# A state-space block with adaptive norms: the input of later halves loaded with channels on partitions and normed in place, the gates' rows moved to other engines, and the output weight's load issued earlier

## The chip, the cores and the metric

The kernel runs on one core of one Trainium2 chip. The metric is device time in microseconds of one execution, all loads and stores included. Three runs of the kernel before the change took 735.45, 736.16 and 738.33 us, so the median is 736.16 us. The profile comes from one more execution on the chip; the predicted time is that of the changed kernel on the same inputs.

## The reference

The input `x` is 4 batches of 512 tokens with 512 channels, all in float32. A conditioning row per batch gives six vectors, and the block adds two branches to `x`, an SSD (Mamba2) mixer and a layer with binarised weights:

```python
mod = (silu(c) @ wmod).reshape(4, 6, 1, -1)
sa, ca, ga, sb, cb, gb = (mod[:, i] for i in range(6))
ga = (2 * (ga >= 0) - 1) * maximum(abs(ga), 0.25)      # gb likewise
h = layernorm(x) * (1 + ca) + sa
x = x + ga * attn(h)
h = layernorm(x) * (1 + cb) + sb
x = x + gb * (h @ (sign(weight) * mean(abs(weight), axis=1, keepdims=True)).T + bias)
```

`attn` projects `h` to 3136 columns: 2048 for x, B and C, 1024 for z, 64 for dt. The 2048 go through a causal convolution of four taps and a silu. Then a scan over chunks of 128 tokens runs for 64 heads of 16 channels and 8 groups with a state of 64: within a chunk `Y_diag = C B^T * exp(segsum(-dt)) * X`, across chunks the carried states times their decays. `D * x / dt` is added, the result is multiplied by `silu(z + z_bias)`, and a projection takes 1024 channels back to 512. All inputs reach the kernel as float32 arrays that the host may lay out anew (transposed, split over partitions), without arithmetic.

## The kernel before

**Tiles.** The 2048 tokens are worked off in eight halves `h` of T = 256 tokens, two to a batch. A half has two chunks of 128 tokens, and each chunk has four pairs of head groups, which makes eight units (h, chunk, pair) in a half. One step of the outer loop (lines 844–863) finishes one unit and begins the one two steps on.

**Stages of a half.** `load_x` (75) brings two tiles of 128 tokens x 512 channels. `f_norm` (307) calls `layer_norm` (289): VectorE takes the statistics (295, 296) and adds the epsilon (297), GpSimd raises to the power −1/2 (298), VectorE normalises in place (300). `f_hT` (335) turns the normed tiles on TensorE (`turned_x`, eight transposes of 128x128, line 330, into two PSUM tiles `phT`), and ScalarE scales and shifts four blocks of 128x256 out of PSUM into `hT` (347). GpSimd fills the three columns ahead of `hT` that the convolution needs. `f_dt` (353) projects the 64 dt columns (`pa`, 368), works out dt and its running sums on VectorE and ScalarE, and writes the sums, their exponentials and the reciprocals to DRAM (`sums_d`, `e_d`, `r_d`). They come back by loads that lay one head's row over all 128 partitions.

`conv_pair` (434–459) projects two blocks of channels (`pp_x`, `pp_B`, `pp_C`, line 434: four matmuls of 128x128 by 259 columns each), takes the last tap on ScalarE (450), the other three on VectorE (454), a tanh on ScalarE (458) and the silu's product on VectorE (459). `f_z` (516–522) does the same for z without a convolution. `f_xt` and `f_Bt` turn x and B to tokens on partitions.

**Units.** Stage 0 loads the sums of one pair of groups into one of four buffers `decay0`–`decay3` (lines 541 and 542, a load of 256 KB and one of 128 KB for each buffer, SP's queue). ScalarE takes exponentials (549), TensorE works out C B^T (`gy`), VectorE masks it (`gm`, 621) and multiplies decay by it (625), and TensorE multiplies the product by x (`py`, 212 and 215, two halves of 16 matmuls each). `pst` is the product for the carried states.

**Tail of a chunk.** `tail1` (739–747) projects back to 512 channels (`po`, 16 matmuls by 512 columns), multiplies by the first gate, adds the input (loaded once more as `xr`) and norms; `tail2` turns and scales; `tail3` (775–779) multiplies by the binarised weight `bwT` (`pf`), by the second gate, adds and stores.

**Once, during the first two halves.** `late_mods` (233) makes the four remaining rows of the modulation in PSUM tile `pg`, copies them to SBUF (243), turns two of them (247, 248) and then computes the gates: five VectorE operations (256–260), the last with the FFN's bias `brow` (loaded on SP, 255), and three writes to `gate_d` in DRAM (262, SP's queue). `load_gates` reads them back over all partitions per batch into `gates`, a tile for which `room` was used before. `load_wout` (264) loads the output weight, 2 MB, after `pg`'s matmuls have read the data whose place it takes. `signs(o)` (269) loads a block of 128 rows of the FFN weight (`fw`, 256 KB), reduces its absolute values to `alpha` (274) and takes signs; `turned_signs(o)` (281) transposes it into `bwT`.

**What sets the order.** The lists FRONT, FIRST and SECOND (787–810) name the step at which each of these functions is called: for halves 2 to 7 the load of x at step 1, the norm at 2, `hT` and dt at 3, B and C from 4, x from 5, z from 8, counted in the units of the half before. `behind` pins a function behind the latest projection of its half on TensorE. Lines 822–829 place `late_mods` at step 1, `load_wout` at 2, `signs(o)` at `o // 2 + 2` and `turned_signs(o)` at `o // 2 + 5`. A scheduler then orders the instructions of each engine from the program's order, priorities and buffers: PSUM tiles come from five "mm" buffers and two others, SBUF tiles from pools (x and xr share three, `hT` has two, `rr` two). Each engine, SP and GpSimd as issuers of DMAs too, works its own list in order and stands where the next instruction isn't ready. All loads named here are issued by SP; the writes of the halves after the first by GpSimd.

Of the kernel before, what the change touches and what calls it, by code (L numbers as in the profile page):

```python
# [11 lines left out]
F32 = mybir.dt.float32  # L12
# [4 lines left out]
P = 128  # L17
# [23 lines left out]
def adaln_mamba_block(  # L41
    ctx: ExitStack,
    tc: tile.TileContext,
    x: bass.AP,
    w_inT: bass.AP,
# [27 lines left out]
    xs_of = {}  # L73

    def load_x(h, queue=nc.sync):
# [5 lines left out]
        xs_of[h] = tiles  # L81

# [37 lines left out]
    sums_d = dram.tile([NHALF, 2, NH, CH], F32, name="sums_d")  # L120
    e_d = dram.tile([NHALF, 2, NH, CH], F32, name="e_d")
# [111 lines left out]
    def late_mods(h):  # L233
# [26 lines left out]
        nc.vector.tensor_mul(ab[second, :], sg[second, :], brow[second, :])  # L260
        for i, v in enumerate((sg[0:B, :], sg[second, :], ab[second, :])):
            nc.sync.dma_start(gate_d[:, i, :], v)
# [26 lines left out]
    def layer_norm(tiles, name, into=None):  # L289
# [3 lines left out]
        rs = wk.tile([P, n], F32, tag=f"rs{n}", name=f"rs_{name}")  # L293
# [4 lines left out]
        nc.gpsimd.tensor_tensor(rs, rs, mhalf[:, :n], ALU.pow)  # L298
        for j, t in enumerate(tiles):
# [5 lines left out]
    H = [dict(B={}, C={}, xt={}, xs={}, bt={}, z={}) for _ in range(NHALF)]  # L305
# [29 lines left out]
    def f_hT(h, turned=None):  # L335
        b = h // HPB

        hT = wk.tile([P, NK, KS - 1 + T], F32, tag="hT", name=f"hT_{h}")
# [4 lines left out]
        for d2 in range(NK // 2):  # L343
# [562 lines left out]
```

## Time and profile before

| what | value |
|---|---|
| median of three runs | 736.16 us |
| profiled execution | 737.38 us, of which 735.7 us are the span of the profile |
| mean granted clock of TensorE | 0.993 |
| instructions | 15007 |
| bytes moved by DMA | 99.24 MB, 135 GB/s in the mean |
| one later half | 86.0 or 87.3 us, in turns |
| ScalarE's decay exponentials (549) | 960 of 395 ns, 293.9 us |
| VectorE's decay products (625) | 120 of 1341 ns, 160.8 us |
| transposes of x on TensorE (330) | 64 of 273 ns |
| normalisations of x (300) | 16, median 546 ns |
| scaling into `hT` (347) | 32, median 564 ns |

The span is the time from the first to the last profiled instruction; 1.7 us of the execution lie outside it. A line of a timeline gives start and duration in microseconds, engine and line of the code, operation, output from inputs, partitions and elements, and how many instructions are put together (xN); in brackets stands the idle time of that engine just before and what ended it. A line of the windows gives the stretch, its length, each engine's busy time and number of instructions, TensorE's granted clock (1.00 is full speed), the mean busy share of the DMA engines and the rate. In the chain of waits each line is a start, a duration and the work that everything after it waited for. PEld is TensorE's weight load, which overlaps its matmuls; SPq is SP's own queue of DMA issues. A line of DMA issues gives the number, the size of each, and the median time from issue to landing.

### The profile page before, as it was taken

What the parts mean: (1) busy time and instruction counts of PE and PEld (TensorE: products, weight loads), DVE (VectorE), ACT (ScalarE), POOL (GpSimd) and SP (SyncE); (2) the same over time, 40 slices, a digit from 0 to 9 for tenths busy, and PEclk for the clock granted to TensorE, in tenths of its full rate; (3) what the DMA queues carried; (4) which work ended last, traced back from release to release, by engine and by line L of the source; (5) the groups of instructions that cost most, each with busy time, mean ns of one, the idle gap of its engine ahead of it and who ended that gap; (6) DMA issues with size and microseconds to landing.
All of it is one profiled execution on the core that took longest, in us unless ns stands there. A gap on an engine that the chain in (4) does not pass through costs nothing.

```text
span 735.7 us, 15007 instructions
## 1 busy us (share of the span) xinstructions
PE 700.4 (95%) x5196; PEld 500.8 (68%) x5196; DVE 599.5 (81%) x1170; ACT 522.0 (71%) x1507; POOL 254.8 (35%) x297
## 2 busy tenths in 40 slices
PE   6999979899999999999999999999999999999997
PEld 3786746666677666677677666776667866677754
DVE  3869888876998678986899768996799867996995
ACT  2467658748696697785976787865968768788941
POOL 4021323444243332343223342433414332333652
PEclk9999989999999999999999999999999999999999
DMA  8991693535555256444644256552564537457720
GB/s 279 328 291 41 204 208 85 135 98 142 127 132 144 63 155 137 102 115 102 159 116 130 53 116 168 142 137 53 140 132 114 130 86 176 116 150 151 142 69 29
DMA packets 119067, 99.24 MB, mean 135 GB/s; under 512 B 73984, under 2 KB 97152, under 8 KB 118992
## 3 DMA queue, kind: packets, MB, share of 16 engines
q1 hardware_dynamic: 117808, 96.39, 52.3%
q0 software_dynamic: 896, 1.38, 0.7%
q8 instruction: 41, 0.67, 0.4%
q10 hardware_dynamic: 288, 0.52, 0.2%
q14 instruction: 34, 0.28, 0.1%
HBM read 92.47 MB, written 5.79 MB: 134 GB/s over the span
## 4 chain that ended last, share of the span: by engine, by line
PE 65%; ACT 16%; DVE 9%; DMA 4%; issue 4%; POOL 1%; SPq 1%; ACTq 0%; DVEq 0%; POOLq 0%
PE po L739 14%; PE pp_x L434 11%; PE pp_z L434 10%; ACT decay L549 9%; PE pp_C L434 7%; PE pp_B L434 5%; PE pf L775 3%; PE py L212 2%; PE py L215 2%; DVE decay L625 2%; ACT h L759 2%; DVE u_x L454 2%; DMA fw<-in_ffn_w 2%; ACT win L549 2%; PE gy L215 2%
## 5 line engine op out<-in xcount | busy, mean ns | idle before, releaser
L549 ACT ACTIVATE decay<-decay,st 128x128 f32<-128x128 f32 x960 | 293.9, 395 | 4.2 <-DMA decay<-sums_d 3.7
L625 DVE SCALAR_TENSOR_TENSOR decay<-decay,gm 128x1024 f32<-128x1024 f32 x120 | 160.8, 1341 | 50.3 <-ACT decay L549 47.2
L434 PE MATMUL pp_x<-hT,win 128*128 128x259 f32 x512 | 120.7, 390 | 7.3 <-DVE u_C L454 7.3
L434 PE MATMUL pp_z<-hT,win 128*128 128x256 f32 x512 | 118.1, 383 | 0.0
L434 PEld LDWEIGHTS pp_x<-hT,win 128*128 128x128 f32 x512 | 96.9, 193 | 25.2 <-ACT decay L549 7.7
L739 PE MATMUL po<-wout,z 128*128 128x512 f32 x256 | 113.8, 595 | 0.0
L434 PEld LDWEIGHTS pp_z<-hT,win 128*128 128x128 f32 x512 | 94.3, 189 | 16.3 <-issue 3.5
L675 POOL TENSOR_TENSOR z<-yt,z 128x256 f32<-128x256 f32 x62 | 62.9, 1015 | 76.1 <-DVE yt L674 57.8
L454 DVE SCALAR_TENSOR_TENSOR u_x<-pp_x,cw,u_x 128x256 f32<-128x256 f32 x192 | 83.6, 474 | 1.3 <-ACT u_x L450 0.7
L739 PEld LDWEIGHTS po<-wout,z 128*128 128x128 f32 x256 | 47.5, 190 | 53.1 <-issue 52.4
L672 POOL TENSOR_TENSOR yt<-yt,xs 128x256 f32<-128x256 f32 x46 | 41.4, 899 | 106.3 <-DVE yt L671 78.6
L507 POOL TENSOR_TENSOR xs<-u_x,rr 128x512 f32<-128x512 f32 x32 | 42.7, 1334 | 79.2 <-DVE u_x L459 61.3
L516 ACT ACTIVATE uz<-pp_z,zb 128x256 f32<-128x256 f32 x64 | 27.5, 470 | 59.0 <-PE pp_z L434 59.0
L215 PE MATMUL py<-decay,xpad 128*32 128x128 f32 x1680 | 66.3, 276 | 0.0
L434 PE MATMUL pp_B<-hT,win 128*128 128x259 f32 x256 | 63.5, 396 | 2.7 <-ACT decay L549 1.9
L434 PE MATMUL pp_C<-hT,win 128*128 128x259 f32 x256 | 59.6, 384 | 1.1 <-DVE u_x L454 1.1
L775 PE MATMUL pf<-bwT,h 128*128 128x512 f32 (+1 forms) x136 | 59.0, 578 | 1.4 <-ACT h L759 1.3
L434 PEld LDWEIGHTS pp_B<-hT,win 128*128 128x128 f32 x256 | 47.4, 193 | 14.5 <-ACT decay L549 3.1
L450 ACT ACTIVATE u_x<-pp_x,cb,cw 128x256 f32<-128x256 f32 x64 | 35.3, 560 | 30.5 <-PE pp_x L434 30.4
L434 PEld LDWEIGHTS pp_C<-hT,win 128*128 128x128 f32 x256 | 47.8, 189 | 9.4 <-PE pn L424 1.4
L679 POOL TENSOR_TENSOR xd<-xpad,st 128x256 f32<-128x256 f32 x48 | 34.1, 727 | 55.8 <-PE pst L215 28.3
L212 PE MATMUL py<-decay,xpad 128*32 128x128 f32 x240 | 47.4, 279 | 3.2 <-issue 2.2
(157 smaller groups left out, 1080.9 us busy)
## 6 DMA issues: line engine op xcount, KB each, us to landing
decay<-sums_d SPq DMA_DIRECT2D x120, 256.0 KB
decay<-sums_d SPq DMA_DIRECT2D x120, 128.0 KB
rr<-r_d SPq DMA_DIRECT2D x64, 128.0 KB
e<-e_d SPq DMA_DIRECT2D x96, 64.0 KB
win<-in_w_inT SPq DMA_DIRECT2D x4, 1024.0 KB
xr<-in_x SPq DMA_DIRECT2D x16, 256.0 KB
res<-o SPq DMA_DIRECT2D x15, 256.0 KB
x<-in_x SPq DMA_DIRECT2D x14, 256.0 KB
```

What stands on the lines that cost most here:

```text
L212: first = products[0]()
L215: product()
L434: last = mm(pm, win[:, k, col : col + P], H[h]["hT"][:, k, lo:], start=(k == 0), stop=(k == NK - 1))
L450: nc.scalar.activation(u[:, j, :], pm[:, KS - 1 :], AF.Identity, bias=cb[:, t : t + 1], scale=cw[:, t, KS - 1 : KS])
L454: nc.vector.scalar_tensor_tensor(u[:, j, :], pm[:, k : k + T], cw[:, t, k : k + 1], u[:, j, :], ALU.mult, ALU.add)
L507: nc.gpsimd.tensor_tensor(xs, xc, rr, ALU.mult)
L549: nc.scalar.activation(ets[r][:, i, :], ets[r][:, i, :], AF.Exp, bias=H[h]["st"][:, hd : hd + 1], scale=-1.0)
L625: nc.vector.scalar_tensor_tensor(ets[r], ets[r], 1.0, bc_mid(gm[:, r, :], HPG), ALU.min, ALU.mult)
L672: ew.tensor_add(t, t, xs)
L675: ew.tensor_mul(zg, t, zg)
L739: last_po = mm(po, H[h]["z"][g // 2][:, g % 2, c * CH : (c + 1) * CH], wout[:, g, :], start=(g == 0), stop=(g == NKI - 1))
L775: mm(pf, h2[:, k, :], bwT[:, k, cols], start=(k == 0), stop=(k == NK - 1))
```

## The change

**The load and the norm.** The host hands over a second copy of the input, `xT`, with channels on partitions. For halves 1 to 7, `load_x` also loads the half's block of it straight into the tile `hT`. `f_norm` then only takes the statistics from the token-major tiles and writes means and factors to a new DRAM array `stat_d`, from GpSimd's queue. `f_hT` reads them back over all partitions (`mr`, 256 KB, SP's queue), subtracts and multiplies in place on VectorE over all four blocks, and ScalarE scales and shifts each block in place. The eight transposes of these halves and their PSUM tiles go. Half 0 keeps its path.

**The gates.** The five VectorE operations become one on VectorE, one on ScalarE and three on GpSimd, called at step 2 as `late_gates`, behind `load_wout` in the program. The three writes to `gate_d` go to GpSimd's queue. `brow` is loaded early with the other late loads, and the tiles lie in `room`.

**The order.** With the gates' writes off SP and `load_wout` ahead of them, the output weight's load is behind `pg`'s matmuls only. `signs` moves from step `o // 2 + 2` to `o // 2 + 4`, `turned_signs` from `o // 2 + 5` to `o // 2 + 6`.

```diff
     def load_x(h, queue=nc.sync):
...
         xs_of[h] = tiles
+        if h > 0:
+            hT = wk.tile([P, NK, KS - 1 + T], F32, tag="hT", name=f"hT_{h}")
+            queue.dma_start(hT[:, :, KS - 1 :], xT[:, :, h * T : (h + 1) * T])
+            H[h]["hT"] = hT
...
+    stat_d = dram.tile([NHALF, 2, T], F32, name="stat_d")
...
+        nc.sync.dma_start(brow[second, :], ffn_b.partition_broadcast(B))
...
-        g = row[0:64, :]
-        sg = wk.tile([64, DM], F32, tag="h2", name="sg")
-        ab = wk.tile([64, DM], F32, tag="h2", name="ab")
-        brow = wk.tile([64, DM], F32, tag="th", name="brow")
-        second = slice(32, 32 + B)
-        nc.sync.dma_start(brow[second, :], ffn_b.partition_broadcast(B))
-        nc.vector.tensor_scalar(sg, g, 0.0, 2.0, ALU.is_ge, ALU.mult)
-        nc.vector.scalar_tensor_tensor(ab, g, -1.0, g, ALU.mult, ALU.max)
-        nc.vector.tensor_scalar(ab, ab, 0.25, None, ALU.max)
-        nc.vector.scalar_tensor_tensor(sg, sg, -1.0, ab, ALU.add, ALU.mult)
-        nc.vector.tensor_mul(ab[second, :], sg[second, :], brow[second, :])
+        late_row.append(row)
+
+    late_row = []
+    second = slice(32, 32 + B)
+    brow = room[0:64, 2, :]
+
+    def late_gates(h):
+        g = late_row.pop()[0:64, :]
+        sg, ab = room[0:64, 0, :], room[0:64, 1, :]
+        nc.vector.tensor_scalar(sg, g, 0.0, 0.5, ALU.is_ge, ALU.subtract)
+        nc.scalar.activation(ab, g, AF.Abs)
+        nc.gpsimd.tensor_scalar(ab, ab, 0.25, 2.0, ALU.max, ALU.mult)
+        nc.gpsimd.tensor_tensor(sg, sg, ab, ALU.mult)
+        nc.gpsimd.tensor_tensor(ab[second, :], sg[second, :], brow[second, :], ALU.mult)
         for i, v in enumerate((sg[0:B, :], sg[second, :], ab[second, :])):
-            nc.sync.dma_start(gate_d[:, i, :], v)
+            nc.gpsimd.dma_start(gate_d[:, i, :], v)
...
     def f_norm(h):
+        ms = wk.tile([P, 2, 2], F32, tag="ms", name=f"ms_{h}")
+        mv = statistics(xs_of.pop(h), f"a{h}", ms[:, 1, :])
+        nc.gpsimd.tensor_copy(ms[:, 0, :], mv[:, :, 0])
+        with nc.allow_non_contiguous_dma(reason="a token's value is on its partition"):
+            nc.gpsimd.dma_start(stat_d[h].rearrange("q (j p) -> p q j", p=P), ms)
+
+    def f_first(h):
         H[h]["xn"] = xs_of.pop(h)
         layer_norm(H[h]["xn"], f"a{h}", H[h]["xn"])
-
-    def f_first(h):
-
-        f_norm(h)
...
     def f_hT(h, turned=None):
...
-        for d2 in range(NK // 2):
-            pt = turned[d2] if turned else turned_x(h, d2)
-            for q in range(2):
-                dt = 2 * d2 + q
-                nc.scalar.activation(
-                    hT[:, dt, KS - 1 :], pt[:, q, :], AF.Identity,
-                    bias=modT[:, 0, dt, b : b + 1], scale=modT[:, 1, dt, b : b + 1],
-                )
-        H[h]["hT"] = hT
+        now = hT[:, :, KS - 1 :]
+        if not turned:
+            mr = wk.tile([P, 2, T], F32, tag="rr", name=f"mr_{h}")
+            nc.sync.dma_start(mr, stat_d[h].partition_broadcast(P))
+            nc.vector.tensor_sub(now, now, bc_mid(mr[:, 0, :], NK))
+            nc.vector.tensor_mul(now, now, bc_mid(mr[:, 1, :], NK))
+        for dt in range(NK):
+            nc.scalar.activation(
+                now[:, dt, :], turned[dt // 2][:, dt % 2, :] if turned else now[:, dt, :], AF.Identity,
+                bias=modT[:, 0, dt, b : b + 1], scale=modT[:, 1, dt, b : b + 1],
+            )
...
             at(2, load_wout)
+            at(2, late_gates, h)
             for o in range(NK):
-                at(o // 2 + 2, signs, o)
+                at(o // 2 + 4, signs, o)
     for o in range(NK):
-        at(o // 2 + 5, behind, 1, turned_signs, o)
+        at(o // 2 + 6, behind, 1, turned_signs, o)
...
         "x": np.ascontiguousarray(np.asarray(L0_attn_input_).reshape(B * L, DM)),
+        "xT": cols(np.asarray(L0_attn_input_).reshape(B * L, DM).T),
```

`statistics` is the first part of the old `layer_norm` (295–298) as a function of its own, which writes the factors into a tile given to it and returns means and variances; `layer_norm` now calls it.

More of the change, by code (lines that the diff above doesn't have):

```diff
@@ L44, in adaln_mamba_block @@
     x: bass.AP,
+    xT: bass.AP,
     w_inT: bass.AP,
@@ L73, in adaln_mamba_block @@
     xs_of = {}
+    H = [dict(B={}, C={}, xt={}, xs={}, bt={}, z={}) for _ in range(NHALF)]
     def load_x(h, queue=nc.sync):
@@ L286, in turned_signs, with statistics @@
         nc.scalar.activation(bwT[:, :, o * P : (o + 1) * P], pt, AF.Copy, scale=2.0 / DM)
-    def layer_norm(tiles, name, into=None):
+    def statistics(tiles, name, rs):
         n = len(tiles)
@@ L298, in layer_norm @@
         nc.gpsimd.tensor_tensor(rs, rs, mhalf[:, :n], ALU.pow)
+        return mv
+    def layer_norm(tiles, name, into=None):
+        n = len(tiles)
+        rs = wk.tile([P, n], F32, tag=f"rs{n}", name=f"rs_{name}")
+        mv = statistics(tiles, name, rs)
         for j, t in enumerate(tiles):
@@ L302, in layer_norm @@
             )
-    H = [dict(B={}, C={}, xt={}, xs={}, bt={}, z={}) for _ in range(NHALF)]
     def f_norm(h):
+        ms = wk.tile([P, 2, 2], F32, tag="ms", name=f"ms_{h}")
[4 more added lines that the diff above has]
+    def f_first(h):
         H[h]["xn"] = xs_of.pop(h)
         layer_norm(H[h]["xn"], f"a{h}", H[h]["xn"])
-    def f_first(h):
-        f_norm(h)
         for xp in xpads:
@@ L336, in f_hT @@
         b = h // HPB
-        hT = wk.tile([P, NK, KS - 1 + T], F32, tag="hT", name=f"hT_{h}")
+        if turned:
+            hT = H[h]["hT"] = wk.tile([P, NK, KS - 1 + T], F32, tag="hT", name=f"hT_{h}")
+        hT = H[h]["hT"]
         if h % HPB == 0:
```

1 line of the change is left out of this document (removed).

## The prediction

> **What bounds the kernel now.** I read the page's busy shares and its chain of waits first:
>
> ```profile
> PE 700.4 (95%) x5196; PEld 500.8 (68%) x5196; DVE 599.5 (81%) x1170; ACT 522.0 (71%) x1507; POOL 254.8 (35%) x297
> ...
> PE 65%; ACT 16%; DVE 9%; DMA 4%; issue 4%; POOL 1%; SPq 1%; ACTq 0%; DVEq 0%; POOLq 0%
> ```
>
> TensorE is the bound: 700.4 of 735.7 us. The change can win the 35 us in which it idles and the time of instructions that go, no more. Then the windows, by stage: the second half's start, and one whole later half (184.2 to 270.2), with the columns PE, PEld, DVE, ACT, POOL, granted clock, DMA share, GB/s.
>
> ```profile
> 84.00:98.00 14.00, 9.93 (x105) 7.99 (x104) 12.16 (x29) 7.54 (x19) 5.82 (x8) 0.99 1.04 279
> 98.00:110.00 12.00, 10.60 (x46) 7.20 (x47) 10.30 (x23) 7.28 (x22) 1.34 (x2) 0.73 0.92 210
> 184.20:249.40 65.20, 64.59 (x432) 46.84 (x430) 59.07 (x122) 47.59 (x137) 20.47 (x23) 1.00 0.47 113
> 249.40:270.20 20.80, 19.93 (x199) 14.04 (x195) 13.39 (x22) 16.96 (x52) 9.52 (x13) 1.00 0.49 124
> ```
>
> In the long projection stretch PE idles 0.61 us of 65.2 and VectorE is busy 59.07 (91%), so VectorE has 6.1 us to spare there. Only the second half's start loses much. The windows of 2 us and the chain say by what:
>
> ```profile
> 96.00:98.00 2.00, 0.00 (x0) 0.00 (x0) 1.68 (x5) 1.20 (x2) 0.00 (x0) 0.91 1.10 281
> 98.00:100.00 2.00, 0.59 (x2) 0.53 (x3) 2.00 (x7) 2.00 (x8) 0.00 (x0) 0.50 1.02 294
> ```
> ```profile
> 83.06 13.38 DMA fw<-in_ffn_w
> ...
> 106.70 7.08 PE po L739 x16
> ```
> ```profile
> 72.66 0.60 SPq L262 DMA_DIRECT2D gate_d<-sg  x2
> ...
> 81.79 0.41 SPq L265 DMA_DIRECT2D wout<-in_w_outT  x1
> ```
>
> The first FFN weight block, issued behind the 2 MB output weight, lands 13.4 us later. VectorE's in-order queue waits on it, and PE stands from 94.05 to 99.41, then runs at a granted clock of 0.50 until about 105. On SP the output weight stood behind the gates' writes, the last at 77.66.
>
> Last, PE's timeline where one half passes into the next:
>
> ```profile
> 179.06 1.09 PE L330 MATMUL phT<-ident,x 128*128 128x128 f32 x8
> 180.99 0.27 PE L212 MATMUL py<-decay,xpad 128*32 128x128 f32 x1 [0.84 <-issue]
> ...
> 181.97 0.44 PE L368 MATMUL pa<-hT,win 128*64 128x128 f32 x4 [0.34 <-ACT hT L347]
> ...
> 184.19 2.02 PE L434 MATMUL pp_B<-hT,win 128*128 128x259 f32 x8
> ```
> ```profile
> 181.50 1.65 DVE L625 SCALAR_TENSOR_TENSOR decay<-decay,gm 128x1024 f32<-128x1024 f32 x1
> ```
>
> The eight transposes and the two gaps after them are 1.09 + 0.84 + 0.34 = 2.27 us. But a py half at 183.25 waits for the decay product that VectorE ends at 183.15, so not all of this is the transposes' own.
>
> **The change part by part.** *Transposes off PE (halves 2 to 7, six passages).* At most 2.27 us each. The last decay exp on ScalarE ends at 181.4, the product at 183.15, both untouched, so the second py half stays near 183.25. Ahead of it two of the eight pp_B matmuls can now run, and pa without its wait; the remaining pp_B ends near 186.5 instead of 187.8. I take −1.3 each: −7.8. Bounds: 0 (the four hT activations, 1.91 us, and the decay exps keep ScalarE's order as the limit) and −2.27.
>
> *VectorE's share.* Per half two 128x512 normalisations go (0.546 each, −1.09); a subtract and a multiply over 128x1024 come. No row has that form; an undelayed 128x1024 product takes 1.22 (L625), a mean one 1.34, two 128x512 sums 1.36. At 1.22 that is 2.44 − 1.09 = +1.35 a half. It falls into the 91% stretch, whose first quarter has VectorE busy 96% (15.57 of 16.20 us from 184.2). PE waits for VectorE there only through the conv, with five PSUM buffers between; I take a third, +0.4, times six: +2.4. Bounds 0 (slack of 6.1 us covers it) and 1.35 (2.2 with both operations at the 1.65 seen above).
>
> *The second half's start.* Before, x was normalised at 75–76.6, transposed, and pa ran at 77.87. Now the order of instructions puts one long chain there: bn_aggr 69.7; GpSimd raises to −1/2 (2.55 us here before, 71.79 to 74.34, 0.71 elsewhere); the new copy (0.19, by the 191 ns of the copy in L342) and ScalarE's Abs with GpSimd's clamp (about 0.7) lie beside it; then the write of means and factors to DRAM, 512 pieces of 4 bytes; then mr's load from SP; subtract, multiply, hT's first activation, pa. The output weight's load is let go at about 69 instead of 81.8, so this write meets it. The same kind of write under that load before:
>
> ```profile
> e_d<-es POOLq DMA_DIRECT2D x1, 64.0 KB, 8.4
> ```
>
> Elsewhere it lands in 1.9 (median of seven). I take 8.4: issue 73.5, landed 82. Bounds 1.8 and 8.5; no row has 4-byte pieces. Then mr, 256 KB, 3.9 to 5.0 by the decay loads in the chain (bounds 1.9 and 8.5, as for the write): 86. Two VectorE passes 2.4, an activation 0.56: pa at about 89. PE's order has nothing to put ahead of it: pt_xt ends at 75.1, so PE idles 13.9 us where it idled 2.8 with its transposes, then runs some 3.3 us more than its time at half clock. Against that, the weight blocks are no longer behind the output weight when asked for: the 5.36 us stop and the 3 us lost at half clock go. Together 11.1 + 3.3 − 8.4 = +6.0; one py half stands behind the output projection now (−0.6): the projection starts at 112.1 instead of 106.7, +5.4. Half of it I expect back, because all four decay exps lie ahead of the gap and VectorE has little queued, so the conv chain enters the next stretch with everything prepared: about +2.5. Bounds −1 (the write at 1.9: 5.4 − 6.5) and +9 (the load at 8, nothing caught up).
>
> Here a row and a rule meet. The row: GpSimd's power took 2.55 us against 0.71 while VectorE ran its gate product and a decay product beside it,
>
> ```profile
> 71.79 2.55 POOL L298 TENSOR_TENSOR rs_a<-rs_a,mhalf 128x2 f32<-128x2 f32 x1
> ```
>
> but DMAs from GpSimd's queue land in 1.9 with VectorE 81% busy. The Trainium skill, "SBUF — State Buffer", section "SBUF: two separate sides", speaks against the new write's queue: descriptors of a GpSimd-issued DMA are written by GpSimd's cores, and VectorE operations that hold the shared port keep them out, 620 ns becoming about 3100. By the page alone the write would come 2.5 us later and the total be 2.5 us higher. I go by the row.
>
> *At no cost.* Gates: VectorE loses 0.68 + 0.41 + 0.67 + 0.99 (L257–L260) and keeps one of 0.42; GpSimd gets about 1.3 + 1.3 + 1.0, ScalarE one Abs; GpSimd is 35% busy and the gates are first read at the output projection (113.8). Should gate_d be late, up to 1 us there. The three gate writes leave SP for GpSimd's queue at 0.5 to 0.8 each. SP: fourteen issues more of 0.4 to 0.6 us, in an engine that mostly waits; mr's wait on SP holds the e and gates loads behind it, used microseconds later, and in halves 2 on the statistics are written long ahead. DMA: 768 KB a half more, 5.4 MB on 99.24, mean share about 0.5; GpSimd: seven copies and writes. If this cover is gone it is the third rival. Signs move two steps later, into stretches that need bwT only at the first FFN.
>
> *Sum.* −7.8 + 2.4 + 2.5 = −2.9. The profiled execution took 737.38 (span 735.7), 1.2 above the median of 736.16: 734.5 from its own time, 733.3 on the median. I say 733.0.
>
> **The rivals.** *One, faster:* VectorE's slack covers the additions and the gap of the second half is short. Six times 2.27 = 13.6, second half at 0: about 722. For it: the 6.1 us of slack, and 2.27 us of PE time that simply goes. Against: the py half bound at 183.25.
>
> *Two, slower:* VectorE becomes the bound of the projection stretch (184–249). The transposes saved give nothing, since conv products set the pace: 6 × 1.3 + 2.5 = +10.3, 746. It decides once the spare 6.1 us of 65.2 can't be used because PE meets a full set of PSUM buffers; for it speaks 96% in the first quarter, against it PE's 0.61 us of idle time.
>
> *Three, slower:* the 512 KB load of hT stands on SP directly ahead of the next decay loads. In the long stretch a busy share of 0.47 moves 113 GB/s, so all queues together move 240, and 512 KB take 2.2 us. If ScalarE waits that long once a half, it costs 6 × 2.2 = 13.2, and 13.2 − 7.8 + 2.4 + 2.5 = +10.3, 746; ScalarE's decay exps are 9% of the chain. It decides where the load is issued less than 2.2 us before the decay load that ScalarE waits for. For it: 4.2 us of ScalarE's idle time is already put down to decay loads; against: only 4.2 in 120.
>
> *Four:* the change doesn't do what it says: PE's time at the passage is not on the path, because ScalarE's decay exps set pp_B's end either way. 0 + 2.4 + 2.5 = 741.
>
> **How the numbers follow.** Forecast 0.46, One 0.18, Two 0.19, Three 0.10, Four 0.07. About 0.5% is what a measurement of this kernel can tell from no change: 732.5 to 739.8. The forecast's own range is 727 to 739 (unknowns: write and load at the second half −3.5 to +6.5, the passages 0 to −2.27): 0.19 of it counts as faster, 0.25 as same, 0.02 as slower. One is faster; Two and Three slower; Four 0.04 slower, 0.03 same. Together 0.37, 0.28, 0.35. The range runs from One's 722 to 748, just beyond Two and Three, which leaves under 2 in 10 out.
>
> **What would show it.** PE's timeline: a gap from about 75 to 89 and a granted clock of 0.50 after it, none at 94–99; the DMA list: the new write's landing (8 us once, about 2 elsewhere); the phT group at 8 instead of 64 matmuls; at the passages pp_B's end 1.3 us earlier against the decay product; in the 65 us stretch VectorE's busy time up 1.35 and PE's idle time by 0.4. The subtract at over 1.6 us, or ScalarE's waits on decay loads well above 4.2 us, would make the forecast wrong; so would a second half whose output projection starts before 107 or after 118.

## The result, and the profile after

The changed kernel takes 775.32 us in the median of four runs (773.78 to 777.69), the kernel before 735.81 beside it: a ratio of 1.054, 95% interval 1.051 to 1.056. The prediction was 733.0 with a range of 722 to 748. The profiled execution took 777.69 us with a span of 775.9, so it is compared with the 735.7 of before: +40.2.

The page of the changed kernel, busy shares, engines of the chain that ended last, and one of its costliest groups:

```profile
PE 701.8 (90%) x5140; PEld 501.2 (65%) x5140; DVE 608.3 (78%) x1166; ACT 525.2 (68%) x1508; POOL 279.9 (36%) x317
...
PE 36%; DVE 21%; ACT 18%; DMA 15%; issue 6%; POOL 4%; SPq 1%; ACTq 0%; DVEq 0%; POOLq 0%
...
L580 ACT ACTIVATE decay<-decay,st 128x128 f32<-128x128 f32 x960 | 293.4, 391 | 37.8 <-DMA decay<-sums_d 37.7
```

56 matmuls fewer, and nearly the same busy time. The chain went from 65% TensorE to 36%; VectorE has 21% of it (9 before) and DMA 15% (4). ScalarE's decay exponentials, which waited 3.7 us for their loads, wait 37.7. The windows of the second half's start:

```profile
75.00:84.00 9.00, 0.00 (x0) 0.00 (x0) 6.04 (x4) 7.36 (x25) 8.30 (x9) 0.56 0.13 44
84.00:98.00 14.00, 6.77 (x30) 5.01 (x31) 6.16 (x11) 3.23 (x7) 0.00 (x0) 0.55 0.71 225
98.00:110.00 12.00, 12.00 (x120) 9.64 (x119) 11.94 (x33) 7.82 (x22) 3.86 (x7) 1.00 0.36 92
```

TensorE does nothing from 74 to 91.2, and the granted clock is 0.56 and 0.55 in the first two stretches. The stop of before at 94 to 99.4 is gone; VectorE is busy all of the third stretch. SP's timeline says what it waits for, and the list of DMA issues how long the new write takes:

```profile
67.92 0.39 SPq L284 DMA_DIRECT2D wout<-in_w_outT  x1
83.17 0.33 SPq L375 DMA_DIRECT2D mr<-stat_d  x1
```
```profile
stat_d<-ms POOLq DMA_DIRECT2D x7, 2.0 KB, 8.9
```

2 KB land after 8.9 us in the median, 8.6 to 11.4 over the six of seven whose landing the trace tells. The chain of waits in a later half shows what hangs on that:

```profile
255.69 8.64 DMA stat_d<-ms
264.38 4.31 DMA mr<-stat_d
268.71 1.24 DVE hT L376
...
277.37 0.94 PE ph L788 x4
```

The write, the read-back, the subtract on VectorE; behind it in VectorE's queue stand a decay product and the norm of the chunk's tail (`t`, `xr`, `st_f`), and TensorE waits 3.6 us for the latter before `ph`, as its timeline says:

```profile
277.37 0.94 PE L788 MATMUL ph<-ident,t 128*128 128x128 f32 x4 [3.64 <-DVE t L325]
```

Its next matmuls run slower too: from 277.3 to 282 the granted clock is 0.64. VectorE's list of waits sums it up (us in total, times, longest), SP's likewise:

```profile
DVE hT L376 <- DMA mr<-stat_d: 23.9, 6, 6.2
```
```profile
SPq L375 <- DMA stat_d<-ms: 52.2, 6, 14.8
```

The span can be cut at the starts of the dt projection (`pa`, the first matmuls that need a half's `hT`) of halves 1, 2 and 7. All tables below use these cuts; the columns are microseconds of the profiled executions, the last one is the median of the timed runs.

| kernel | to half 1 | half 1 to 2 | 2 to 7 (five halves) | 7 to end | span | median |
|---|---|---|---|---|---|---|
| before | 77.9 | 104.1 | 431.6 | 122.1 | 735.7 | 735.8 |
| after | 91.2 | 108.4 | 451.0 | 125.3 | 775.9 | 775.3 |
| difference | +13.3 | +4.3 | +19.4 | +3.2 | +40.2 | |

Half of the loss lies in the five steady halves, 3.9 us a half in the mean, most of the other half in the second half (17.6 us up to the start of half 2), and 3 us at the end. The five are far from equal: they lose 5.4, 3.4, 4.3, −0.8 and 7.1 us, and VectorE's waits before the subtract in them are 5.4, 0, 5.7, 0.9 and 6.2 us. In the second of them, where VectorE doesn't wait, a decay load takes 11.1 us (shown below with the write).

### The profile page after: what moved, and what is told of

It reads as the page before. It is cut to its first block, busy times and chain, and to the rows that moved or that the text cites. A ratio compares the mean times of both kernels' runs of the same rounds, so it can differ in the third digit from the quotient of the medians.

```text
span 775.9 us, 14958 instructions
## 1 busy us (share of the span) xinstructions
PE 701.8 (90%) x5140; PEld 501.2 (65%) x5140; DVE 608.3 (78%) x1166; ACT 525.2 (68%) x1508; POOL 279.9 (36%) x317
## 4 chain that ended last, share of the span: by engine, by line
PE 36%; DVE 21%; ACT 18%; DMA 15%; issue 6%; POOL 4%; SPq 1%; ACTq 0%; DVEq 0%; POOLq 0%
ACT decay L580 10%; DMA decay<-sums_d 6%; PE pp_z L465 6%; PE pf L806 5%; DVE decay L656 5%; PE pp_x L465 4%; PE pp_C L465 4%; PE po L770 4%; DMA stat_d<-ms 3%; PE pp_B L465 3%; DMA mr<-stat_d 2%; DVE u_x L485 2%; ACT win L580 2%; DVE u_B L485 2%; PE py L226 2%
## 5 line engine op out<-in xcount | busy, mean ns | idle before, releaser
L580 ACT ACTIVATE decay<-decay,st 128x128 f32<-128x128 f32 x960 | 293.4, 391 | 37.8 <-DMA decay<-sums_d 37.7
L656 DVE SCALAR_TENSOR_TENSOR decay<-decay,gm 128x1024 f32<-128x1024 f32 x120 | 159.7, 1332 | 41.4 <-ACT decay L580 40.2
L465 PE MATMUL pp_z<-hT,win 128*128 128x256 f32 x512 | 120.0, 387 | 0.0
L465 PEld LDWEIGHTS pp_z<-hT,win 128*128 128x128 f32 x512 | 95.9, 192 | 17.1 <-issue 3.6
L706 POOL TENSOR_TENSOR z<-yt,z 128x256 f32<-128x256 f32 x62 | 58.1, 938 | 106.8 <-DVE yt L705 88.1
L703 POOL TENSOR_TENSOR yt<-yt,xs 128x256 f32<-128x256 f32 x46 | 46.9, 1020 | 118.1 <-DVE yt L702 79.9
L485 DVE SCALAR_TENSOR_TENSOR u_x<-pp_x,cw,u_x 128x256 f32<-128x256 f32 x192 | 85.4, 476 | 3.2 <-ACT u_x L481 2.4
L770 PEld LDWEIGHTS po<-wout,z 128*128 128x128 f32 x256 | 47.6, 190 | 53.3 <-issue 52.7
L226 PE MATMUL py<-decay,xpad 128*32 128x128 f32 x1680 | 68.9, 284 | 0.0
L538 POOL TENSOR_TENSOR xs<-u_x,rr 128x512 f32<-128x512 f32 x32 | 46.0, 1439 | 58.3 <-DVE u_x L490 54.1
L465 PEld LDWEIGHTS pp_B<-hT,win 128*128 128x128 f32 x256 | 47.7, 194 | 17.7 <-ACT h L790 4.1
L710 POOL TENSOR_TENSOR xd<-xpad,st 128x256 f32<-128x256 f32 x48 | 38.4, 814 | 54.6 <-ACT xpad L524 32.1
L223 PE MATMUL py<-decay,xpad 128*32 128x128 f32 x240 | 48.9, 287 | 1.7 <-DVE decay L656 1.0
L226 PEld LDWEIGHTS py<-decay,xpad 128*32 128x32 f32 x1680 | 49.7, 113 | 0.2
```

What stands on the lines that cost most here:

```text
L223: first = products[0]()
L226: product()
L465: last = mm(pm, win[:, k, col : col + P], H[h]["hT"][:, k, lo:], start=(k == 0), stop=(k == NK - 1))
L485: nc.vector.scalar_tensor_tensor(u[:, j, :], pm[:, k : k + T], cw[:, t, k : k + 1], u[:, j, :], ALU.mult, ALU.add)
L538: nc.gpsimd.tensor_tensor(xs, xc, rr, ALU.mult)
L580: nc.scalar.activation(ets[r][:, i, :], ets[r][:, i, :], AF.Exp, bias=H[h]["st"][:, hd : hd + 1], scale=-1.0)
```

## The experiments

### One part at a time

The gates' part alone: the kernel before with `late_gates`, `load_wout` ahead of it, and signs two steps later; and the other part alone.

```diff
# gates_only, against before
+            at(2, late_gates, h)
-                at(o // 2 + 2, signs, o)
+                at(o // 2 + 4, signs, o)
# xT_only, against after: the same lines put back
```

> The kernel before with the second half of the change alone: gates' rows on other engines, the output weight's load ahead of them, signs two steps later; x is normed and transposed as before. Theory A, that the whole loss lies in the new path of hT: the 5.4 us stop behind the weight loads and about 3 us at half clock go, nothing new is waited for, 727 to 733 us. Theory B, that the loss lies in the early output weight and the gates on GpSimd (the gate rows reach DRAM late, the early 2 MB load delays others): slower than 740 us.

> The changed kernel with the gates, the output weight and the signs put back as before: only the loads of hT from the transposed input, the statistics through DRAM and the norm in place are left. Theory A (the loss is the hT path's): 765 to 785 us, with ScalarE's waits for decay loads near 38 us as in the changed kernel. Theory B (the loss is the gates' part): 730 to 742 us.

| kernel | to half 1 | half 1 to 2 | 2 to 7 | 7 to end | span | median | ratio to before |
|---|---|---|---|---|---|---|---|
| gates_only | 76.1 | 107.9 | 431.7 | 123.0 | 738.7 | 742.4 | 1.008 (1.006 to 1.011) |
| xT_only | 97.7 | 102.2 | 460.7 | 125.7 | 786.3 | 785.2 | 1.065 (1.061 to 1.069) |

gates_only falls where theory B had it, and xT_only where theory A had it (0.2 us above its range; ScalarE's waits for decay loads are 46 us): both parts lose alone, 49.0 and 6.3 us, and together 39.5. The hT path carries the loss, and the gates' part takes 10 us off it; but it is no gain by itself. TensorE's idle times in gates_only, from its timeline:

```profile
99.43 3.06 PE L444 MATMUL pp_x<-hT,win 128*128 128x259 f32 x8 [3.69 <-DVE u_C L464]
...
118.84 0.63 PE L767 MATMUL ph<-ident,t 128*128 128x128 f32 x4 [1.79 <-DVE t L310]
...
132.95 1.36 PE L444 MATMUL pp_x<-hT,win 128*128 128x259 f32 x5 [3.91 <-ACT xpad L503]
```

The stop at 99.4 was 5.36 us behind the weight blocks. With these out of the way it is still 3.69: here the chain of waits runs almost wholly over VectorE's dt and conv steps from 85 to 99.4, which the wait for the DMA had hidden, as far as this one run tells. The output projection starts 2.6 us earlier than in the kernel before. And from the first output projection to the second it takes 52.7 us (104.0 to 156.7) where it took 47.7. One more run put the signs back:

> The gates' part alone (as in the run of it that took 742.4 us), with signs and turned signs at their old steps. If the later signs cost the 5 us between the first two output projections, where ScalarE then has the decay exponentials, the FFN's scaling and the signs' scaling in one stretch: 728 to 735 us. If GpSimd's gate operations or the early output weight cost it: 740 to 744 us.

742.4 us again (1.008, 1.006 to 1.010): 51.9 us between the two projections. The later signs are not the cause; whether GpSimd's gate operations or the early 2 MB load is, these runs don't tell.

### The write: its pieces, its wait, its queue

```diff
# e16, against after
-    stat_d = dram.tile([NHALF, 2, T], F32, name="stat_d")
+    stat_d = dram.tile([NHALF, P, 2, 2], F32, name="stat_d")
...
-            nc.gpsimd.dma_start(stat_d[h].rearrange("q (j p) -> p q j", p=P), ms)
+            nc.gpsimd.dma_start(stat_d[h], ms)
# and the subtract and multiply read mr with a step of 16 bytes
# nowait, against after
-            nc.sync.dma_start(mr, stat_d[h].partition_broadcast(P))
+            nc.sync.dma_start(mr, w_inT[h, 0 : 2 * T].rearrange("(q t) -> q t", q=2).partition_broadcast(P))
# actq, against after
-            nc.gpsimd.dma_start(stat_d[h].rearrange("q (j p) -> p q j", p=P), ms)
+            nc.scalar.dma_start(stat_d[h].rearrange("q (j p) -> p q j", p=P), ms)
```

> The changed kernel with one size changed: the statistics go to DRAM as 128 pieces of 16 bytes (both values of both tokens of a partition side by side) instead of 512 of 4, and are read back in the same one load of 256 KB; every engine's order is unchanged. Theory A, that the small pieces set the write's 8.9 us and hold up all other loads meanwhile: landing falls to 2 to 4 us, ScalarE's waits for decay loads from 38 to under 20 us, time 745 to 760 us. Theory C, that the round trip's place in the queues costs the time whatever the write takes: landing may fall, the time stays above 768 us.

> The changed kernel, but what is subtracted and multiplied is read from a row of the projection weight that waits for nothing (so the norm is left out and the result is not the reference's); the statistics are still taken and written in 512 pieces. All engines' orders stay. Theory C, that the wait for the write costs the time (SP, VectorE and TensorE stand behind it): the gap of 17 us in the second half shrinks below 8 and the total falls to 735 to 748 us. Theory A, that the write itself holds up the decay loads that are under way at the same time: ScalarE's waits for decay loads stay above 20 us and the total above 752 us.

> The changed kernel with the write of the statistics, still 512 pieces of 4 bytes, issued from ScalarE's queue in place of GpSimd's; TensorE, VectorE and SP keep their orders. If GpSimd's queue makes the write slow: landing 2 to 4 us and the total near the 751.6 us of the 16-byte kernel. If the pieces do: landing 8 us or more and the total 765 to 785 us.

| kernel | to half 1 | half 1 to 2 | 2 to 7 | 7 to end | span | median | ratio to before |
|---|---|---|---|---|---|---|---|
| after | 91.2 | 108.4 | 451.0 | 125.3 | 775.9 | 775.3 | 1.054 (1.051 to 1.056) |
| e16 | 88.9 | 102.8 | 432.7 | 126.3 | 750.7 | 751.6 | 1.021 (1.019 to 1.023) |
| nowait | 87.5 | 108.2 | 436.7 | 127.0 | 759.4 | 761.7 | 1.035 (1.033 to 1.037) |
| actq | 95.7 | 101.4 | 461.4 | 126.2 | 784.7 | 786.9 | 1.070 (1.067 to 1.073) |

e16 changes the size of the pieces and no engine's order, and takes back 23.7 us, as theory A had it; of the spans' difference 18.3 us lie in the steady halves, which are then within 1.1 us (0.2 a half) of the kernel before. It does so although its subtract and multiply, with the step of 16 bytes, take 2.0 to 2.1 us each in place of 1.23. Its write and ScalarE's waits:

```profile
DMA to landing us min/median/max: 2.1/3.3/5.1
```
```profile
ACT decay L580 <- DMA decay<-sums_d: 16.9, 11, 3.1
```

nowait keeps the 512 pieces and every engine's order, and removes the dependency on them (its read-back takes a row of the projection weight). Theory C's signs stay out: the gap is 13.9 us and the total 761.7; theory A's both come. Yet nowait gets back 14.3 of the steady halves' 19.4 us, so 14.3 is what waiting for the write costs there; the other 5.1 hold the write's presence and the rest of the change, of which e16 leaves 1.1. ScalarE's waits for decay loads hardly fall there:

```profile
ACT decay L580 <- DMA decay<-sums_d: 33.4, 14, 7.4
```

How a write of 2 KB holds up others is seen in the changed kernel. The write is issued at 342.1, the loads of two decay buffers (768 KB) from 343.70; the chain and the windows (last column GB/s):

```profile
344.24 11.14 DMA decay<-sums_d
```
```profile
343.00:345.00 2.00, 2.00 (x43) 1.60 (x43) 2.00 (x6) 2.00 (x8) 0.98 (x1) 1.00 0.30 43
345.00:347.00 2.00, 2.00 (x11) 1.76 (x10) 1.88 (x4) 1.31 (x4) 2.00 (x4) 1.00 2.44 31
347.00:349.00 2.00, 2.00 (x13) 1.74 (x13) 1.90 (x4) 0.62 (x2) 1.92 (x3) 1.00 0.52 25
349.00:351.00 2.00, 2.00 (x11) 1.76 (x10) 0.69 (x1) 0.74 (x2) 0.98 (x2) 1.00 0.66 16
351.00:353.00 2.00, 2.00 (x12) 1.58 (x11) 0.00 (x0) 0.00 (x0) 0.81 (x1) 1.00 0.24 31
353.00:355.00 2.00, 2.00 (x6) 0.83 (x5) 0.00 (x0) 0.00 (x0) 0.00 (x0) 1.00 0.82 215
```

Until the write lands at 350.9, and for two microseconds more, the queues move 16 to 43 GB/s with 768 KB asked for; from 353 on 215. A decay load that took 3.9 to 5.0 us in the chain of the kernel before takes 11.1.

actq speaks against the queue: from ScalarE's queue the write is no faster. Between its issue and the issue of the read-back that waits for it lie 8.9, 9.8 and 9.0 us in halves 3, 4 and 5 (252.65 to 261.53, 342.54 to 352.35, 439.37 to 448.37). The list of DMA queues shows the pieces there: 3984 packets on queue q10, which has 288 in the changed kernel, so 528 more for each of the seven writes, its 512 pieces and 16 besides. Why actq is 11.6 us slower than the changed kernel is not shown. Two more runs add the write to the kernel before, where nobody reads it and no engine's order changes:

```diff
# before_w4, against before; before_w16 has stat_d as [NHALF, P, 2, 2] and writes mv as it lies
+        if h > 0:
+                nc.gpsimd.dma_start(stat_d[h].rearrange("k p -> p k"), mv.rearrange("p j q -> p (j q)"))
```

> The kernel before with one thing more: behind the statistics of halves 1 to 7, GpSimd writes them to DRAM in 512 pieces of 4 bytes, and nobody reads them. All engines' orders are those of the kernel before. If such a write holds up the other loads for its 9 us (as the rate of 20 GB/s during it suggests): ScalarE's waits for decay loads rise from 4 to 15 us or more and the total by 8 to 25 us, 744 to 761. If it costs nobody but its own reader: 735 to 739 us.

> As the run before it, with 128 pieces of 16 bytes. If the number of pieces is what counts: landing 2 to 5 us and the total 736 to 741 us. If any additional write from GpSimd's queue at this place holds up the loads: as long as with 4 bytes.

739.6 us (1.0055, 1.004 to 1.007) with 512 pieces, 736.2 (1.000, 0.999 to 1.002) with 128. The landings of the one and the other:

```profile
DMA to landing us min/median/max: 8.7/9.2/10.6
```
```profile
DMA to landing us min/median/max: 1.8/2.0/3.0
```

So how the 2 KB are cut sets the landing, in every half and with nobody waiting; whether by the number of the pieces or by their size, these two don't tell. Holding up others costs about 4 us in the old order (0.0055 of 736; 3 to 5 by the interval); its steady halves lose nothing in the profiled execution (431.6 us). ScalarE waits 9.0 us for decay loads there, 2.4 with 128 pieces and 3.7 in the kernel before. The 15 us of waits and the 8 us in total that were expected were too many, but it is not free either. What the write costs is above all the wait for it, in a place where VectorE stands in line.

### The round trip through TensorE instead

```diff
# pe_stat, against after (pe_xT the same against xT_only)
+            mr = ps.tile([P, 2, T], F32, tag="mm", name=f"mr_{h}")
+                    mm(mr[:, q, j * CH : (j + 1) * CH], ms[:, q, j : j + 1].to_broadcast([P, P]), ident, start=True, stop=True)
```

> The changed kernel without the round trip through DRAM: four fp32 matmuls of 128x128 lay each token's mean and factor over all partitions in a PSUM tile, and the subtract and the multiply read them there. Everything else of the change stays; the scheduler moves some instructions. If the round trip (its small pieces, SP's and VectorE's waits for it) is the whole loss: ScalarE's waits for decay loads fall from 38 us to under 10, the 17 us gap of the second half falls under 4, total 730 to 744 us. If loads with channels on partitions (512 KB more per half) or VectorE's two passes cost by themselves: 748 us or more.

> As the run before it, with the gates, the output weight and the signs put back as in the kernel before. If the norm in place without the round trip saves 1.3 us a half on TensorE as the prediction had it: 726 to 732 us. If VectorE's additional 1.4 us a half eat that: 734 to 741 us. If the order of gates and signs costs the 6 us that the gates' part alone cost, this run lies about 6 us under the one with the gates' part.

| kernel | to half 1 | half 1 to 2 | 2 to 7 | 7 to end | span | median | ratio to before |
|---|---|---|---|---|---|---|---|
| pe_stat | 77.9 | 109.6 | 473.2 | 122.0 | 782.7 | 785.2 | 1.066 (1.062 to 1.069) |
| pe_xT | 81.9 | 108.5 | 471.4 | 122.3 | 784.1 | 785.4 | 1.067 (1.064 to 1.069) |

Without any round trip the second half's gap is gone as expected (77.9), and yet the kernel is slower than the changed one: the steady halves lose 8.3 us each in the mean. The first theory falls for the total. The second had the total, but not its reason: e16 has the same loads and longer passes on VectorE, and its steady halves lose 0.2. What differs is the order: the scheduler had moved the norm. In the changed kernel the subtract stands at 268.7 with `pa` at 290.0; here it stands at 278.9 with `pa` at 282.9, in the middle of the passage. VectorE's and TensorE's timelines of pe_stat there:

```profile
278.90 1.20 DVE L377 TENSOR_TENSOR hT<-hT,mr 128x1024 f32<-128x1024 f32 x1
```
```profile
278.10 0.30 PE L222 MATMUL py<-decay,xpad 128*32 128x128 f32 x1 [1.46 <-DVE decay L657]
...
282.87 2.17 PE L400 MATMUL pa<-hT,win 128*64 128x128 f32 x16 [4.13 <-ACT hT L380]
```

TensorE waits 1.5 us for the decay product ahead of them and 4.1 for hT behind them. Another kernel shows the same in its own way (e16_h2 below: with the read-back in other buffers the scheduler places it late in halves 2 to 7; 837.5 us, gaps of 10 to 13 us before each of their `pa`).

### The second half's gap

```diff
# e16_h2, against e16
-            mr = wk.tile([P, P, 2, 2], F32, tag="rr", name=f"mr_{h}")
+            mr = wk.tile([P, P, 2, 2], F32, tag="h2", name=f"mr_{h}")
# e16_first, against e16: h2 in the second half only, and there
+          with tc.high_priority(offset=400) if h == 1 else nullcontext():
# around the read-back, the subtract, the multiply and the scaling
```

> The kernel with 16-byte pieces, with the read-back tile in other buffers (those of h2 in place of those of rr); in the second half only the buffer changes, later halves are ordered anew in part. If the load of the read-back waits in the second half for GpSimd's product on the rr buffers (it was issued at 80.9 us there, when that product ended, though the write had landed by 76.5): it is issued at 72 to 77 us and the first dt matmul runs at 83 to 86 instead of 88.9 us. If it waits for the write: issued at 80 us or later again.

> The 16-byte kernel (751.6 us) with the second half's norm given priority and the read-back tile there in h2's buffers: on VectorE the subtract and multiply stand behind one decay product instead of four, on ScalarE hT behind two decay loads' exponentials instead of four, on SP the read-back ahead of the output weight. If their place behind the decay work, more than the write or the buffer, made the second half's gap of 15.3 us: the gap falls to 3 to 8 us, the first dt matmul runs at 78 to 83 instead of 88.9 us, the total at 741 to 748. If the write's landing or the read-back makes it: gap above 12 us.

In e16_h2 the read-back is issued at 76.67 in place of 80.88, as the buffer theory said, and `pa` starts at 88.7 in place of 88.9. The wait was real and worth nothing, for VectorE has something else first (its timeline):

```profile
82.05 2.04 DVE L656 SCALAR_TENSOR_TENSOR decay<-decay,gm 128x1024 f32<-128x1024 f32 x1 [0.16 <-ACT decay L580]
84.02 1.96 DVE L376 TENSOR_TENSOR hT<-hT,mr 128x1024 f32<-128x1024 f32 x1
```

The subtract follows the fourth decay product at once. In e16_first it stands behind one:

```profile
71.95 1.23 DVE L658 SCALAR_TENSOR_TENSOR decay<-decay,gm 128x1024 f32<-128x1024 f32 x1 [1.20 <-ACT decay L582]
79.47 1.97 DVE L377 TENSOR_TENSOR hT<-hT,mr 128x1024 f32<-128x1024 f32 x1 [6.29 <-DMA mr<-stat_d]
```

`pa` starts at 84.1 and the gap is 9.8 instead of 15.3 (expected were 3 to 8), now behind the read-back. The total is 750.4 us (1.020, 1.018 to 1.022), above the 741 to 748 expected and 1.2 us under e16: of the 4.8 us won at 84, 2.1 are lost again by half 2 (104.9 against 102.8), and 2.4 are left in the span. Most of what is won at the start of this half isn't kept.

### The steady halves

```diff
# e16_late, against xT_only: 16-byte pieces, and
-        if h > 0:
+        if h > 1:
# (half 1 normed and transposed as before); late_nonorm, against e16_late
-            nc.sync.dma_start(mr, stat_d[h].partition_broadcast(P))
-            nc.vector.tensor_sub(nj, nj, ...)
-            nc.vector.tensor_mul(nj, nj, ...)
```

> 16-byte pieces, the new path in halves 2 to 7 only, half 1 normed and transposed as before, and gates, output weight and signs as before. If the 10 us that the 16-byte kernel lost in the second half and the gates' part are all that is left: 736 to 742 us. If the prediction's -1.3 us a half is there once nothing hides it: 728 to 734 us. If the steady halves cost by themselves: 745 us or more.

> 16-byte pieces, new path in halves 2 to 7 only, gates as before (742.6 us), with the read-back, the subtract and the multiply left out of those halves (so the norm is left out and the result is not the reference's); statistics and their write stay. If VectorE's two passes (3.9 us a half there) and the wait for the read-back eat the 1.3 us a half that the transposes' absence gives: 728 to 736 us. If nothing of the transposes' time lies on the path anyway: 738 to 743 us.

| kernel | to half 1 | half 1 to 2 | 2 to 7 | 7 to end | span | median | ratio to before |
|---|---|---|---|---|---|---|---|
| before | 77.9 | 104.1 | 431.6 | 122.1 | 735.7 | 735.8 | |
| e16_late | 76.5 | 106.2 | 431.0 | 126.7 | 740.4 | 742.6 | 1.009 (1.006 to 1.012) |
| late_nonorm | 76.5 | 99.9 | 430.9 | 125.7 | 733.0 | 737.4 | 1.002 (1.000 to 1.005) |

e16_late lies 0.6 us above the first of its ranges; late_nonorm falls between its two, with executions from 734.3 to 742.5 us, of which the profiled one (734.7) is among the fastest, and with parts of the engines' orders changed. The prediction had 1.3 us off each passage and 0.4 us on each half. Without the transposes the five halves take 0.6 us less in all; with VectorE's passes and the read-back left out as well, 0.7. The windows over exactly these five halves, of the kernel before, of late_nonorm and of the changed kernel:

```profile
182.00:613.60 431.60, 423.60 (x3174) 305.97 (x3174) 360.47 (x707) 321.08 (x935) 149.85 (x178) 1.00 0.49 119
```
```profile
176.40:607.30 430.90, 418.51 (x3140) 301.36 (x3136) 352.20 (x699) 321.18 (x937) 162.31 (x186) 1.00 0.50 125
```
```profile
199.60:650.60 451.00, 425.65 (x3140) 306.51 (x3136) 369.56 (x709) 325.41 (x943) 164.12 (x186) 0.98 0.52 123
```

TensorE's busy time falls by 5.1 us (the transposes), the stretch by 0.7: the rest turns into idle time, 8.0 before and 12.4 then. TensorE's list of waits shows it growing ahead of `pn`, the matmuls that turn the running sums of dt: 5.3 us in four waits where before has 0.4 in one. An engine that is busy 98% of a stretch does not set its length alone here. The changed kernel has late_nonorm's 3140 matmuls, yet TensorE is busy 7.1 us longer in them, at a clock of 0.98 against 1.00; of the 20.1 us between the two, 13.0 are idle time and 7.1 matmuls at a lower clock. Leaving the norm out gives 6 us once, at the first passage (99.9 against 106.2), and nothing in the five after it.

### SP's order

In the changed kernel the scheduler also put loads of `rr` ahead of decay loads on SP, where they wait for the write of `r_d`: 69.9 us in nine waits, 3.2 in one before. Four runs took these loads to GpSimd's queue:

```diff
-            nc.sync.dma_start(
+            (nc.gpsimd if h else nc.sync).dma_start(
                 rr[:, r, :],
```

> The changed kernel with the loads of rr (reciprocals read back from DRAM) of halves 1 to 7 on GpSimd's queue in place of SP's. In the changed kernel SP stood 70 us in all before rr loads until the write they read had landed (3 us in the kernel before), with decay loads queued behind them. If that order is a large part of the 39 us: SP's wait goes, ScalarE's waits for decay loads fall from 38 to under 20 us, total 755 to 765 us. If the small pieces alone are the cause: 770 us or more.

> The 16-byte kernel (751.6 us) with the rr loads on GpSimd's queue. If SP's 71 us before rr loads cost the 4 to 5 us that the last half lost and part of the rest: 742 to 748 us, ScalarE's waits for decay loads under 8 us (17 before). If they cost nothing: 750 to 754 us.

> 16-byte pieces, new path in halves 2 to 7 only, gates as before (742.6 us), with the rr loads on GpSimd's queue. If the last half's 5 us come from SP's order: 734 to 739 us. If they come from elsewhere: 741 to 744 us. Under 732 it would beat the kernel before.

> The kernel before with the rr loads on GpSimd's queue, the control for the three others: with SP standing 3 us only before these loads, 734 to 738 us; slower than 740 us if GpSimd's queue itself costs.

| kernel | to half 1 | half 1 to 2 | 2 to 7 | 7 to end | span | median | without the edit |
|---|---|---|---|---|---|---|---|
| before_rrq | 78.0 | 105.4 | 434.6 | 124.5 | 742.5 | 743.2 | 735.8 |
| after_rrq | 90.3 | 109.8 | 464.6 | 125.2 | 789.9 | 792.0 | 775.3 |
| e16_rrq | 89.4 | 101.7 | 441.2 | 126.4 | 758.7 | 751.8 | 751.6 |
| late_rrq | 76.6 | 109.7 | 432.5 | 125.0 | 743.8 | 745.0 | 742.6 |

(The profiled execution of e16_rrq was the slowest of its four, which span 749.4 to 760.4.) The control is slower by itself (1.009, 1.007 to 1.011), so the edit costs about 6 us there, and none of the others gains. The scheduler also ordered the engines anew in part, so the totals don't tell what SP's waits cost. The waits say more, in after_rrq most plainly: SP's waits for `r_d` fall from 69.9 us to 4.8, and ScalarE's waits for decay loads are what they were (37.7):

```profile
ACT decay L580 <- DMA decay<-sums_d: 36.9, 16, 8.3
```

In the other two pairs they stay as well, 16.9 and 17.8 us (e16, e16_rrq), 12.2 and 12.7 (e16_late, late_rrq). This speaks against the theory that SP's `rr` waits make the decay loads late. The last half stays open: it takes 125.0 in late_rrq against 126.7 without the edit, but 124.5 in the control.

## Why the prediction was wrong

*What bounds the kernel.* "TensorE is the bound": its 95% of the span was read as a limit. late_nonorm speaks against it in the steady halves, with 5.1 us less work and 0.7 us less time.

*Transposes off TensorE, −1.3 a passage.* Measured −0.1 a half (e16_late and late_nonorm). The bound of 0 that the prediction named was the value; its reason there, other engines' order as the limit, fits the idle time that grew ahead of `pn`; which of ScalarE and VectorE sets it was not tried.

*VectorE's share, +0.4 a half.* The durations were right, 1.226 us each against an assumed 1.22. Unwaited they cost nothing in the steady halves of e16_late. What was left out is that they wait: VectorE stood 23.9 us before the read-back in six halves, with a decay product and the tail's norm queued behind.

*The step that failed.* Under "at no cost": "in halves 2 on the statistics are written long ahead". They are written 13 us before the subtract (255.69 to 268.71), and 8.6 + 4.3 us of that are the write and the read-back. The landing of 1.9 us "elsewhere" was a row of another kind, 64 KB in 128 rows of 512 bytes; 2 KB in 512 pieces take 8.6 to 11.4, and before_w4 shows this in every half, not only under the output weight's load. The steady halves' +3.9 in the mean is this step (e16: +0.2; nowait: 14.3 us of the 19.4 from the wait).

*The second half.* Its chain was right in its parts: the read-back issued at 83.17 (82 forecast), 4.9 us long (4), `pa` at 91.2 (89), the output projection at 113.3 (112.1). That the write's price came near is partly luck: the forecast put its 8.4 us (11.4 measured) down to the output weight's load, and before_w4 has 10.6 at this place, ahead of that load, and 8.7 to 9.7 in the later halves. And e16_h2 shows that a quick write alone would have changed little, since the subtract stood behind four decay products; the prediction had these as a help ("all four decay exps lie ahead of the gap"). Wrong was "half of it I expect back": from that projection to the next it takes 61.8 us against 47.7, so that at half 2 the loss is 17.6 instead of 2.5. It takes 62.0 in nowait too, 55.6 in e16 and 52.7 in gates_only: the small pieces and the gates' part each have a share in these 14 us, and what the rest is stays open. And of the 8.4 us that the weights' early load was to give, gates_only shows 1.7 at the stop itself, 2.6 by the output projection, and a loss in the end.

*The rivals.* None was it. The third rival named a symptom that came, ScalarE waiting for decay loads, but put it on the 512 KB loads of hT; e16 has the same loads and half the waits (16.9). The second rival's place, VectorE's queue, was right, but as waiting, not as work. The fourth had the transposes at nothing, as was measured, but not the loss. For the steady halves all four priced work and transfers; none priced a round trip's latency in an in-order queue.

*The queue of the write.* The prediction set a row against the Trainium skill, "SBUF — State Buffer", section "SBUF: two separate sides", by which a DMA issued from GpSimd may wait for its descriptors while VectorE holds a port that they share. actq speaks against this as the cause: from ScalarE's queue the write takes as long. The rule that did bear is missing from the prediction: the skill's "DMA: Bandwidth & Descriptors", section "Rules for kernel authors", says that a non-contiguous last dimension becomes one descriptor per element and should be rearranged to be contiguous. The 528 packets of each write in actq, against 512 values, agree with it; its price here is before_w4's 9.2 us against before_w16's 2.0.

*Open.* The last half is 3 to 5 us longer in the changed kernel and in those that keep most of its order (125.0 to 127.0 against 122.1), and 122.0 to 122.8 in pe_stat, pe_xT and e16_h2, which are ordered otherwise. It is not the norm's work (late_nonorm 125.7); whether SP's `rr` waits have a part in it these runs don't tell. What makes the gates' part slow between the first two output projections is open too. No kernel of these beats the one before.

## What to carry to other kernels

Before moving work to a detour through DRAM, count the pieces of its writes and add up issue, landing and read-back as a latency; then look at what stands behind the first instruction that waits for it on an in-order engine, because that is what is delayed. Take a busy share near 100% as the bound only where shortening that engine's work has been seen to shorten the stretch. When a kernel is ordered by a scheduler, an experiment that changes a buffer or a dependency can move the very instruction under test: compare the orders first, and trust most the edits that leave them alone (here e16, nowait, before_w4 and before_w16).

## What the runs showed of the hardware that was not expected

- A write of 2 KB in 512 pieces of 4 bytes takes 8.4 to 11.4 us from issue to landing (shortest in after_rrq, longest in the changed kernel), the same bytes in 128 pieces of 16 bytes 1.8 to 6.1 (before_w16, e16_rrq), from GpSimd's queue; from ScalarE's queue the 4-byte form is no faster (8.9 to 9.8 us to the release of its reader in three halves of actq).
- While the 4-byte write is under way, other loads can nearly stand: 16 to 43 GB/s with 768 KB outstanding at 343 to 353 us of the changed kernel, 215 GB/s after that.
- A subtract of 128x1024 takes VectorE 1.23 us with a contiguous second operand (the changed kernel and nowait) and 1.97 to 2.10 with one that steps by 16 bytes (e16).
